# A four-layer graph kernel: later stages' constants are asked for later in the GpSimd queue

## The chip, the cores and the metric

The kernel runs on one core of one Trainium2 chip. A time is the device time of one execution in microseconds (us). Times of the kernel before are given as the median of three runs.

## The reference

There are 2708 tokens with 256 features and a dense 2708 x 2708 matrix `adj` with weights. Four layers follow one another, each of them a graph step and a feed-forward step, both added to `x`:

```
# layer 0
x = x + weights(adj) @ (layernorm(x) @ W + B)      # weight of an entry r: exp(-2 (1/r - 1)^2) where r < 1, else 0
x = x + top-2-of-8 experts(layernorm(x))           # gate: xf @ Wg + bg
# layer 1
x = x + relu(Dinv (adj + I) Dinv @ (layernorm(x) @ W) + b)
x = x + one-of-8 output experts(gelu(layernorm(x) @ W1 + b1))
# layer 2
x = x + elu(one-head attention over adj > 0: h = layernorm(x) @ W.T, scores from attn_src, attn_dst)
x = x + layernorm(two of 8 experts, the same for all tokens) with gamma, beta
# layer 3
x = x + elu(four-head attention over adj > 0, scores from a_l, a_r)
x = x + layernorm(x) @ weight.T + bias
```

All is float32.

## The kernel before

The tokens are 22 tiles of 128 rows (the last one has 20). `x` stays in on-chip memory throughout. A framework (Tile) takes the instructions in the order in which Python emits them, but it lays out the order of each engine's instructions itself, at compile time[...]. An instruction whose inputs are there may so be issued long before its neighbours in the source. `tc.add_manual_dep(... NoSync ...)` is a hint for this planner alone: "put this instruction behind that one on its engine's queue". [...]

**Queues.** Big loads (rows of `adj`, the weights of experts, `x`, `xT`) are asked for by SP (SyncE). Small constants, and all gathers and scatters of token rows (lines 505, 519 and 659), are asked for by GpSimd (POOL): `row_bc` (line 121) loads one vector of 256 numbers into all 128 partitions, 128 KB in all; `mat` (line 127) loads a small matrix. [...]

**The graph step of layer 0.** It begins the program. `centre(w_sb)` subtracts the column means from the layer's matrix (two products, four records on PE, lines 245 and 247). The output tokens are taken in three groups, `GROUPS`, of 9, 7 and 6 tiles. For each group and each of 21 row blocks j, SP loads a row block of `adjT` (`adrow`, line 903, five buffers), `weigh` turns it into weights `wt` with ScalarE and VectorE in turn (lines 141, 887 and 889; four buffers), and PE multiplies them with `msg` (line 931). In the first group, at each even j, `front(j)` also makes `msg` of two tiles: it loads their columns of `xT` (line 871, two buffers) and their rows of `x` (line 56), takes their mean and variance (lines 186 and 187), multiplies them by the layer's matrix (line 260) and writes `msg` (line 878). At j = 19 of the first group `last_rows` fills a buffer with ones on POOL (line 299) and loads the 20 last rows into it. `send` follows each group: it norms the tokens, takes the gate's product with `L0_ffn_Wg` (line 846) and `L0_ffn_bg` (line 848), and scatters the rows to their experts (line 505).

**The rest.** The experts of layer 0 run from about 270 us to 600 us. Layer 1 has the same shape (groups `GROUPS1`; `send1` writes each token's rank with a scatter, kept in `scattered["taken1"]`); its output experts are run by `work1` in blocks, each with a gather of names, a gather of rows, PE products (line 721), two VectorE instructions (lines 722 and 723) and a scatter into `given1`. `beside(b)` runs beside block b. At b = NA + 4 = 13 it asks for layer 2's constants `L2_gnn_attn_src`, `L2_gnn_attn_dst` and `w_l2`; at b = NA + 9 = 18 it notes the latest scatter as `work1.at_end`, and layer 2's other constants (`L2_ffn_Wr`, `br`, `b1`, `b2`, `gamma`, `beta`, and the matrix of layer 3) are put behind that scatter on POOL. Layer 2 then loads `given1` back (`mine`, line 56) once all scatters have landed. Layer 3's `a_r` and `a_l` are emitted in layer 2's first attention pass.

The constants of later stages that the source emits at the start, or that have no hint, are asked for by POOL as soon as their buffer is there.

Of the kernel before, what the change touches and what calls it, by code (L numbers as in the profile page):

```python
# [15 lines left out]
P = 128  # L16
N = 2708
D = 256
DC = D // P
E = 8  # L20
# [8 lines left out]
GROUPS = [range(0, 9), range(9, 16), range(16, NT)]  # L29
# [37 lines left out]
def adj_ffn4(ctx: ExitStack, tc: tile.TileContext, a: dict, out: bass.AP):  # L67
    nc = tc.nc
    v, s, g, te = nc.vector, nc.scalar, nc.gpsimd, nc.tensor
# [54 lines left out]
    def mat(pool, name, n):  # L124

        t = pool.tile([P, DC, n], F32, name=name, bufs=1)
        g.dma_start(t, a[name].rearrange("(c p) n -> p c n", p=P))
        return t
# [18 lines left out]
    def after(i, past):  # L147

        tc.add_manual_dep(i.ins, past, mybir.DependencyInfo(
            mybir.DependencyClass.NoSync, mybir.DependencyReason.DATA), reason="order")  # L150

    def in_order(first, engines):

        was = {}
        for i in nc.cur_bb.bb.instructions[first:]:
            if i.engine in engines:
                if i.engine in was:
                    tc.add_manual_dep(i, was[i.engine], mybir.DependencyInfo(
                        mybir.DependencyClass.NoSync, mybir.DependencyReason.DATA), reason="order")
                was[i.engine] = i.name  # L160
# [135 lines left out]

    def last_rows(dst, parts, filler):

        filler.memset(dst, 1.0)
        for q, k, c0, w in parts:  # L300
            nc.sync.dma_start(dst[q * Q : q * Q + LAST, k : k + w],
                              a["adjT"][FULL * P :, c0 : c0 + w])

    def last_product(p, q, weights, k, values, stop=True):
        te.matmul(p, lhsT=weights[q * Q : q * Q + LAST, k : k + P],
# [194 lines left out]
    scattered = {}  # L500
# [271 lines left out]
    ep = ctx.enter_context(tc.tile_pool(name="early", reuse_waits="tile", bufs=1))  # L772
# [14 lines left out]
    with ExitStack() as l0:  # L787
# [20 lines left out]
        w_sb = gp.tile([P, DC, D], F32, name="L0_gnn_W", bufs=1)  # L808
        first = nc.sync.dma_start(w_sb, a["L0_gnn_W"].rearrange("(c p) n -> p c n", p=P))
        b_bc = row_bc(gp, "L0_gnn_B", D)  # L810
        wg = mat(tp, "L0_ffn_Wg", E)
        bg = row_bc(tp, "L0_ffn_bg", E)
        w_l1 = mat(ep, "L1_gnn_W", D)
        b_l1 = row_bc(ep, "L1_gnn_b", D)
        choice = tp.tile([P, NT, 2], I32, name="choice", bufs=1)
        g.iota(choice, pattern=[[2 * P, NT], [1, 2]], base=0, channel_multiplier=2)
        msg = gp.tile([P, NT, D], F32, name="msg", bufs=1)
# [73 lines left out]
        for tiles in GROUPS:  # L891
            end = tiles is GROUPS[-1]
            own = [(t, (t - tiles[0]) * P, P) for t in tiles if t < FULL]
            c0, w = tiles[0] * P, own[-1][1] + P
            pairs = banks(tiles)
            acc = [gsum.tile([P, 2, D], F32, name="acc2", bufs=(GMAX + 1) // 2) for _ in pairs]

            places = {n: (n // 2 % 4, n // 8 * 2 + n % 2) for n in range(len(own))}
            begin = tiles is GROUPS[0]
            for j in range(FULL):  # L900
                r = rows(j)
                ad = gp.tile([P, GMAX * P], F32, name="adrow", bufs=5)[:r, :w]
                i = nc.sync.dma_start(ad, a["adjT"][j * P : j * P + r, c0 : c0 + w])
                after(i, reads[-1] if reads else first.ins.name)
                reads.append(i.ins.name)
                if begin and j % 2 == 0:
                    if j == 6:
                        centre(w_l1)
                    for t0 in (j,) if j < FULL - 3 else (j, j + 2) if j == FULL - 3 else ():
                        front(t0)  # L910
                if begin and j == FULL - 2:
                    spread_out(msg[:, FULL, :])
                if j == (FULL - 2 if begin else 12):
                    cols = [gp.tile([P, GMAX * P], F32, name=name, tag=name, bufs=bufs)[
                        :, : (1 + max(k for _, k in places.values())) * P]
                            for name, bufs in (("adrow", 5), ("y", 3), ("wt", 4))]
                    last_rows(cols[0], [(places[n][0], places[n][1] * P, c0 + n * P,
                                         min(2, len(own) - n) * P) for n in range(0, len(own), 2)], g)
                    weigh(*cols, P)
                    for n, t, _ in by_turns(own):  # L920
                        last_product(acc[n // 2][:, n % 2, :], places[n][0], cols[2],
                                     places[n][1] * P, msg[:, FULL, :], False)
                y = gp.tile([P, GMAX * P], F32, name="y", bufs=3)[:r, :w]
                wt = gp.tile([P, GMAX * P], F32, name="wt", bufs=4)[:r, :w]
                weigh(ad, y, wt, r)
                for p, pair in zip(acc, pairs):
                    for n in pair:
                        if n == len(own):
                            continue
                        _, k, q = own[n]  # L930
                        te.matmul(p[:q, n - pair[0], :], lhsT=wt[:, k : k + q],  # L931
                                  rhs=msg[:r, j, :], start=(j == 0 and n == pair[0]),
                                  stop=(j == FULL - 1 and n == pair[-1]))
                if end and j == 2:
                    cols = [gp.tile([P, GMAX * P], F32, name=name, tag=name, bufs=bufs)[
                        :, : NT * Q].rearrange("p (t c) -> p t c", c=Q)
                            for name, bufs in (("adrow", 5), ("y", 3), ("wt", 4))]
                    last_columns(cols[0])
                    weigh(*cols, P)
                    last = last_sums(acc[-1].rearrange("p k d -> p (k d)"), cols[2],  # L940
                                     lambda j, r: msg[:r, j, :], D)
                    v.tensor_tensor(x[:LAST, FULL, :], x[:LAST, FULL, :], last, ALU.add)
                if end and j == 0:
                    items = [(early, b, past0, taken[0][: 2 * held0], True) for b in range(N0)]
                    for item in items:
                        work0.fetch_rows(item)
                if end and j in (8, 14):
                    work0.fetch(items[j // 6 - 1])
                if end and j == NT - 5:
                    past = list(scattered["taken0"])  # L950
                    items += [(full, b, past, taken[0][: 2 * held], True) for b in range(NA - N0)]
            for p, pair in zip(acc, pairs):
                if pair[0] == len(own):
                    continue
                t, m, q = own[pair[0]][0], len(pair), own[pair[-1]][2]
                v.tensor_tensor(x[:q, t : t + m, :], x[:q, t : t + m, :], p[:q, :m, :], ALU.add)
            if end:
                sums.close()
                gnn.close()
                psum_pool(l0, 2, 3)  # L960
                hc = l0.enter_context(
                    tc.tile_pool(name="c0", side="right", reuse_waits="tile", bufs=1))
                hcs.append(hc)
                own_rows.append(behind_gate.enter_context(
                    tc.tile_pool(name="x0", reuse_waits="tile", bufs=1)))
                work0.late = hc
                work0.begun = work0.turn(hc, work0.rows[0])
                work0.made = work0.first_products(hc, work0.ahead[0], work0.begun, 2)
            send(tiles)
            if begin:  # L970
                early = blocks(hw, tp, known, N0, 2 * P, "E", full=True)
                past0 = list(scattered["taken0"])
            if tiles is GROUPS[-2]:
                full = blocks(hw, tp, known, NA - N0, 2 * P, "A", done=early[2], full=True)
# [10 lines left out]
        past = list(scattered["taken0"])  # L985
# [60 lines left out]
    with ExitStack() as l1:  # L1046
# [171 lines left out]
        def beside(b):  # L1218
            if b == NA + 9:
                work1.at_end = scattered["given1"][-1].name  # L1220
            if b == NA + 4:
# [5 lines left out]
                score_columns(w_l2, D, as_bc, 1, D)  # L1227
                score_columns(w_l2, D, ad_bc, 1, D + 1)
                centre(w_l2)
                for i in nc.cur_bb.bb.instructions[first:]:  # L1230
                    if i.engine in (mybir.EngineType.DVE, mybir.EngineType.PE):
                        tc.add_manual_dep(i, work1.last, mybir.DependencyInfo(
                            mybir.DependencyClass.NoSync, mybir.DependencyReason.DATA),
                            reason="order")

        work1 = Units(hw, given[1], weights1, hid)
        for tiles in GROUPS1:
# [138 lines left out]
    with tc.tile_pool(name="t3", reuse_waits="tile", bufs=1) as t3:  # L1376
# [34 lines left out]
        with tc.tile_pool(name="g2", reuse_waits="tile", bufs=1) as gp:  # L1411
# [110 lines left out]
            for n in (5, 5, 5, 4, 2):  # L1522
# [20 lines left out]
                if c0 == 0:  # L1543
# [1 line left out]
                    score_columns(wa, D, row_bc(work, "L3_gnn_a_r", D, "elu_e"), NH, D)  # L1545
                    score_columns(wa, D, row_bc(work, "L3_gnn_a_l", D, "elu_e"), NH, D + NH)
                    centre(wa)
                    for i in nc.cur_bb.bb.instructions[begin:]:
                        if i.engine == mybir.EngineType.DVE:
                            tc.add_manual_dep(i, spread, mybir.DependencyInfo(  # L1550
                                mybir.DependencyClass.NoSync, mybir.DependencyReason.DATA),
                                reason="order")

                    es = gp.tile([P, NT, Q], F32, name="es")
                    v.tensor_tensor(es[:, :FULL], Rb[:, None, N - Q : N].to_broadcast([P, FULL, Q]),
# [511 lines left out]
```

## Time and profile before

| | |
|---|---|
| median of 3 runs | 1903.86 us (1902.37 to 1904.59) |
| the profiled execution | 1902.01 us, its span 1900.2 us |
| PE (matmul) busy | 1821.4 us, 96% of the span |
| PE busy in 0 to 140 us, the first group | 128.36 us |
| PE busy in 1050 to 1080 us, the end of layer 1 | 19.62 us |
| POOL busy | 352.3 us, 19% |

Busy shares are averages over stages; the views of a stretch of time tell what a stage waits for. In a view by stretches each engine has its busy time and, in brackets, how many instructions began there; the last columns are the granted clock of TensorE, the busy share of the 16 DMA engines and the GB/s that they moved. Of the DMA queues, q1 holds what SP asks for and q0 what POOL asks for.

### The profile page before, as it was taken

How to read it: one execution, taken by the hardware profiler on the slowest of the kernel's cores; microseconds unless marked ns; L12 is line 12 of the kernel's file. 1: busy time of each engine (PE TensorE's matmuls, PEld its weight loads, DVE VectorE, ACT ScalarE, POOL GpSimd, SP SyncE). 2: the span in 40 equal slices, each digit the busy share in tenths (PEclk: the TensorE clock that was granted, in tenths of full speed). 3: DMA queues.
4: the chain of work that ended last, by engine and by line, in shares of the span. 5: the costliest groups of instructions: out<-in, count | busy, mean ns of one | idle time of the engine just before them, and what ended most of it. 6: DMA issues, size and time to landing. Idle time of an engine off the chain costs nothing.

```text
span 1900.2 us, 25781 instructions
## 1 busy us (share of the span) xinstructions
PE 1821.4 (96%) x9453; PEld 1325.5 (70%) x9453; DVE 1094.9 (58%) x2489; ACT 642.2 (34%) x1448; POOL 352.3 (19%) x415
## 2 busy tenths in 40 slices
PE   7999999999998999999989799998899999999998
PEld 6888788888887888887778688887566722232344
DVE  6777873443333524454532365555345499999897
ACT  7868752222223203022322232223233551131231
POOL 1004254333321002304356410000000000000000
PEclk9999999999998999999999899999899999999999
DMA  8435657877764453644777510000101000000000
GB/s 274 144 110 154 224 194 283 344 298 297 284 256 138 140 151 105 159 117 121 207 224 251 163 29 1 1 1 1 44 1 34 17 1 23 23 15 26 21 20 16
DMA packets 88846, 233.33 MB, mean 123 GB/s; under 512 B 18015, under 2 KB 44679, under 8 KB 80648
## 3 DMA queue, kind: packets, MB, share of 16 engines
q1 hardware_dynamic: 71752, 189.18, 30.4%
q0 software_dynamic: 16960, 42.42, 7.0%
q8 instruction: 78, 1.28, 0.3%
q14 instruction: 56, 0.46, 0.1%
HBM read 216.29 MB, written 28.71 MB: 129 GB/s over the span
## 4 chain that ended last, share of the span: by engine, by line
PE 39%; DVE 4%; DMA 4%; issue 1%; ACT 1%; POOL 1%; POOLq 0%; SPq 0%; DVEq 0%; ACTq 0%
PE num L1965 10%; PE ps_acc L1538 9%; PE den L1975 5%; PE ps_tmp L367 4%; PE ps_acc L1728 3%; PE yacc L721 2%; PE ps_tmp L260 2%; DVE e L1935 1%; DMA names<-taken,b_ix 1%; DMA L_ffn_beta<-in_L_ffn_beta 1%; PE ps_acc L260 1%; PE ps_acc L670 1%; DMA mine<-given 1%; PE ps_tmp L213 0%; DMA hs<-hid,names 0%
## 5 line engine op out<-in xcount | busy, mean ns | idle before, releaser
L1935 DVE SCALAR_TENSOR_TENSOR e<-arena,G,mask 128x1024 f32<-128x1024 f32 (+1 forms) x264 | 286.9, 1147 | 13.7 <-PE den L1975 13.6
L1965 PE MATMUL num<-e,wh 128*64 128x512 f32 (+4 forms) x1056 | 215.3, 551 | 0.3 <-ACT L_gnn_W L1358 0.3
L1538 PE MATMUL ps_acc<-hh,e 128*128 128x257 f32 x882 | 199.2, 382 | 1.7 <-ACT o L1481 1.7
L1302 PE MATMUL acc<-sup,adrow 128*128 128x256 f32 x882 | 199.6, 384 | 1.1 <-DVE adrow L1270 1.1
L931 PE MATMUL acc<-msg,wt 128*128 128x256 f32 x882 | 198.9, 382 | 1.3 <-DVE wt L889 1.2
L1302 PEld LDWEIGHTS acc<-sup,adrow 128*128 128x128 f32 x882 | 166.2, 191 | 29.0 <-issue 5.5
L931 PEld LDWEIGHTS acc<-msg,wt 128*128 128x128 f32 x882 | 165.8, 191 | 27.5 <-DVE wt L889 1.8
L1538 PEld LDWEIGHTS ps_acc<-hh,e 128*128 128x128 f32 x882 | 163.7, 190 | 29.2 <-ACT o L1481 4.3
L583 PE MATMUL ps_acc<-xTs,wa 128*128 128x256 f32 (+1 forms) x768 | 169.3, 373 | 2.1 <-DVE xTs L573 2.0
L617 PE MATMUL yacc<-wb,hTs 128*128 128x256 f32 x736 | 168.4, 380 | 0.0
L585 ACT ACTIVATE hTs<-ps_acc,wa 128x256 f32<-128x256 f32 (+1 forms) x192 | 88.9, 465 | 234.2 <-PE yacc L617 160.0
L583 PEld LDWEIGHTS ps_acc<-xTs,wa 128*128 128x128 f32 x768 | 136.4, 190 | 28.1 <-DVE xTs L573 4.5
L1965 PEld LDWEIGHTS num<-e,wh 128*64 128x64 f32 (+1 forms) x1056 | 66.6, 136 | 127.2 <-issue 105.0
L617 PEld LDWEIGHTS yacc<-wb,hTs 128*128 128x128 f32 x736 | 137.1, 190 | 17.9 <-DVE ys L619 0.5
L1530 DVE SCALAR_TENSOR_TENSOR e<-Rb,G,mask 128x640 f32<-128x640 f32 (+2 forms) x110 | 85.0, 775 | 91.0 <-PE ps_acc L1538 90.4
L1975 PE MATMUL den<-e,wh 128*32 128x512 f32 (+4 forms) x1056 | 118.0, 548 | 0.0
L1267 DVE TENSOR_SCALAR mask<-adrow 128x1024 uint8<-128x1024 f32 (+1 forms) x66 | 41.2, 625 | 122.6 <-DMA adrow<-in_adjT 122.2
L214 ACT COPY xT<-ps_tmp 128x256 f32<-128x256 f32 x76 | 26.8, 367 | 219.9 <-PE ps_tmp L213 219.7
L721 PE MATMUL yacc<-wb,hTs 128*128 128x256 f32 x384 | 87.8, 383 | 0.5 <-DMA wb<-in_L_ffn_Wdp 0.5
L889 DVE SCALAR_TENSOR_TENSOR wt<-adrow,wt 128x640 f32<-128x640 f32 (+3 forms) x67 | 71.0, 1063 | 26.8 <-ACT wt L141 26.4
L1975 PEld LDWEIGHTS den<-e,wh 128*32 128x32 f32 (+1 forms) x1056 | 30.2, 108 | 77.9 <-issue 73.8
L505 POOL DMA_INDIRECT given<-ys,xs x46 | 65.3, 1420 | 79.3 <-DVE ys L620 66.1
(464 smaller groups left out, 2581.8 us busy)
## 6 DMA issues: line engine op xcount, KB each, us to landing
adhalf<-in_adjT SPq DMA_DIRECT2D x42, 677.0 KB
wb<-in_L_ffn_W2p SPq DMA_DIRECT2D x24, 1152.0 KB
wb<-in_L_ffn_Wdp SPq DMA_DIRECT2D x24, 1152.0 KB
wa<-in_L_ffn_W1b SPq DMA_DIRECT2D x24, 1028.0 KB
adrow<-in_adjT SPq DMA_DIRECT2D x42, 512.0 KB
adrow<-in_adjT SPq DMA_DIRECT2D x42, 320.0 KB
adrow<-in_adjT SPq DMA_DIRECT2D x21, 576.0 KB
adrow<-in_adjT SPq DMA_DIRECT2D x21, 448.0 KB
```

Of the source, the lines that this page charges most:

```text
L367: te.matmul(p[:, :w], lhsT=w1[:, c, f * P : (f + 1) * P], rhs=xnT[:, c, c0 : c0 + w], start=(c == 0), stop=(c == DC - 1))
L583: i = te.matmul(p[:, f % 2, : m * P], lhsT=w1[:, c, f * P : (f + 1) * P], rhs=xT[:, c, : m * P], start=(c == 0), stop=(c == DC - 1))
L585: s.activation(hT[:, f, : m * P], p[:, f % 2, : m * P], AF.Gelu, bias=bias[:, f : f + 1])
L617: te.matmul(q[:, k, :], lhsT=hT[:, f, k * P : (k + 1) * P], rhs=w2[:, f, :], start=(f == 0), stop=(f == HC - 1))
L721: te.matmul(q, lhsT=hT[:, f, :], rhs=w2[:, f, :], start=(f == 0), stop=(f == HC - 1))
L931: te.matmul(p[:q, n - pair[0], :], lhsT=wt[:, k : k + q], rhs=msg[:r, j, :], start=(j == 0 and n == pair[0]), stop=(j == FULL - 1 and n == ...
L1302: te.matmul(p[:q, n - pair[0], :], lhsT=ad[:, k : k + q], rhs=sup[:, jj, :], start=(jj == 0 and n == pair[0]), stop=(jj == FULL - 1 and n ...
L1530: i = v.scalar_tensor_tensor(e[:r, :w], Rb[:r, c0 : c0 + w], G[:r, j, :], mask[:r, j, c0 : c0 + w], op0=ALU.max, op1=ALU.mult)
L1538: te.matmul(p[:, : D + 1], lhsT=e[:, k : k + q], rhs=hh[:, j, :], start=(j == 0), stop=False)
L1935: v.scalar_tensor_tensor(e[:, :w], slow[:, m % 2, k, :w], G[:, j, 2 * pair + k, :], mask[:, j, c0 : c0 + w], op0=ALU.max, op1=ALU.mult)
L1965: te.matmul(num[k * DK : (k + 1) * DK, hf, :q], lhsT=wh[some, j, 2 * pair + k, :DK], rhs=e[some, h0 - c0 : h0 - c0 + q], start=(j == 0), s ...
L1975: te.matmul(den[z : z + Q, :q], lhsT=wh[some, i, 2 * pair + k, DK : DK + 1] .to_broadcast([some.stop - some.start, Q]), rhs=e[some, h0 - c ...
```

## The change

A helper `engine_after(first, engine, past)` puts all instructions of one engine that were emitted since `first` behind the instruction `past`, with the same planner's hint. It is used to move nine loads of constants:

- `L0_ffn_Wg`, `L0_ffn_bg`, `L1_gnn_W` and `L1_gnn_b` are emitted at j = 19 of the first group and put behind the fill of `last_rows`, which now returns its name. `centre(w_l1)` moves from j = 6 of the first group to j = 6 of the second.
- `L2_gnn_attn_src`, `L2_gnn_attn_dst` and `w_l2` are put behind the first scatter of ranks of layer 1.
- `L3_gnn_a_r` and `L3_gnn_a_l` are put behind `work1.at_end`.

```
+    def engine_after(first, engine, past):
+
+        for i in nc.cur_bb.bb.instructions[first:]:
+            if i.engine == engine:
+                tc.add_manual_dep(i, past, mybir.DependencyInfo(
+                    mybir.DependencyClass.NoSync, mybir.DependencyReason.DATA), reason="order")
...
     def last_rows(dst, parts, filler):
 
-        filler.memset(dst, 1.0)
+        i = filler.memset(dst, 1.0)
...
+        return i.ins.name
...
         b_bc = row_bc(gp, "L0_gnn_B", D)
-        wg = mat(tp, "L0_ffn_Wg", E)
-        bg = row_bc(tp, "L0_ffn_bg", E)
-        w_l1 = mat(ep, "L1_gnn_W", D)
-        b_l1 = row_bc(ep, "L1_gnn_b", D)
...
+                if tiles is GROUPS[1] and j == 6:
+                    centre(w_l1)
                 if begin and j % 2 == 0:
-                    if j == 6:
-                        centre(w_l1)
...
-                    last_rows(cols[0], ...)
+                    filled = last_rows(cols[0], ...)
+                    if begin:
+                        later = len(nc.cur_bb.bb.instructions)
+                        wg = mat(tp, "L0_ffn_Wg", E)
+                        bg = row_bc(tp, "L0_ffn_bg", E)
+                        w_l1 = mat(ep, "L1_gnn_W", D)
+                        b_l1 = row_bc(ep, "L1_gnn_b", D)
+                        engine_after(later, mybir.EngineType.Pool, filled)
...
-                for i in nc.cur_bb.bb.instructions[first:]:
-                    if i.engine in (mybir.EngineType.DVE, mybir.EngineType.PE):
...
+                for e in (mybir.EngineType.DVE, mybir.EngineType.PE):
+                    engine_after(first, e, work1.last)
+                engine_after(first, mybir.EngineType.Pool, scattered["taken1"][0].name)
...
-                    for i in nc.cur_bb.bb.instructions[begin:]:
-                        if i.engine == mybir.EngineType.DVE:
...
+                    engine_after(begin, mybir.EngineType.DVE, spread)
+                    engine_after(begin, mybir.EngineType.Pool, work1.at_end)
```

More of the change, by code (lines that the diff above doesn't have):

```diff
@@ L916, in adj_ffn4 @@
                             for name, bufs in (("adrow", 5), ("y", 3), ("wt", 4))]
-                    last_rows(cols[0], [(places[n][0], places[n][1] * P, c0 + n * P,
-                                         min(2, len(own) - n) * P) for n in range(0, len(own), 2)], g)
+                    filled = last_rows(cols[0], [(places[n][0], places[n][1] * P, c0 + n * P,
+                                                  min(2, len(own) - n) * P)
+                                                 for n in range(0, len(own), 2)], g)
+                    if begin:
[5 more added lines that the diff above has]
+                        engine_after(later, mybir.EngineType.Pool, filled)
                     weigh(*cols, P)
@@ L1229, in beside @@
                 centre(w_l2)
-                for i in nc.cur_bb.bb.instructions[first:]:
-                    if i.engine in (mybir.EngineType.DVE, mybir.EngineType.PE):
-                        tc.add_manual_dep(i, work1.last, mybir.DependencyInfo(
-                            mybir.DependencyClass.NoSync, mybir.DependencyReason.DATA),
-                            reason="order")
+                for e in (mybir.EngineType.DVE, mybir.EngineType.PE):
+                    engine_after(first, e, work1.last)
+                engine_after(first, mybir.EngineType.Pool, scattered["taken1"][0].name)
         work1 = Units(hw, given[1], weights1, hid)
@@ L1547, in adj_ffn4 @@
                     centre(wa)
-                    for i in nc.cur_bb.bb.instructions[begin:]:
-                        if i.engine == mybir.EngineType.DVE:
-                            tc.add_manual_dep(i, spread, mybir.DependencyInfo(
-                                mybir.DependencyClass.NoSync, mybir.DependencyReason.DATA),
-                                reason="order")
+                    engine_after(begin, mybir.EngineType.DVE, spread)
+                    engine_after(begin, mybir.EngineType.Pool, work1.at_end)
                     es = gp.tile([P, NT, Q], F32, name="es")
```

## The prediction

> **What bounds the kernel now.** I read the page first, then PE's waits, then the stretches of time around the places that the nine moved loads leave and go to. The page says that PE is the engine to watch:
>
> ```profile
> PE 1821.4 (96%) x9453; PEld 1325.5 (70%) x9453; DVE 1094.9 (58%) x2489; ACT 642.2 (34%) x1448; POOL 352.3 (19%) x415
> ```
>
> Only PE's idle time can be won, 79 us of the span. The loads leave the first ten microseconds, so I asked for PE's waits in 0 to 140 us (line, releaser, us in total, times, longest):
>
> ```profile
> PE ps_tmp L260 <- DMA xT<-in_xT: 6.9, 1, 6.9
> PE ps_tmp L245 <- DMA L_gnn_W<-in_L_gnn_W: 3.8, 1, 3.8
> ```
>
> One wait of 6.9 us stands out: the first products of tiles 2 and 3 wait for their columns of `xT`. Next the stretches of 5 us (PE, PEld, DVE, ACT, POOL busy, clock, DMA share, GB/s):
>
> ```profile
> 0.00:5.00 5.00, 1.25 (x3) 1.10 (x4) 0.82 (x28) 1.28 (x1) 4.34 (x15) 1.00 0.55 194
> 5.00:10.00 5.00, 4.48 (x10) 2.60 (x9) 1.56 (x6) 2.42 (x2) 2.91 (x7) 1.00 0.98 282
> 10.00:15.00 5.00, 0.10 (x1) 0.00 (x0) 4.42 (x14) 4.48 (x6) 0.00 (x0) 1.00 0.99 328
> 15.00:20.00 5.00, 3.05 (x7) 2.51 (x8) 3.24 (x6) 2.85 (x3) 0.00 (x0) 1.00 1.02 392
> 20.00:25.00 5.00, 5.00 (x18) 4.11 (x18) 3.64 (x5) 5.00 (x8) 0.00 (x0) 1.00 0.89 274
> ```
>
> From 5 to 20 us the DMA engines are full, and PE does 7.6 us of work in 15. From 20 us on PE is full; from 20 to 200 us it is idle for 0.6 us. So the program's head is bound by DMA, and what follows by PE. Who uses the full DMA engines? The queue rows (packets, MB, share), of 5 to 10 us and then of 10 to 15 us:
>
> ```profile
> q1 hardware_dynamic: 595, 1.10, 59.8%
> q0 software_dynamic: 153, 0.31, 38.5%
> ```
>
> ```profile
> q0 software_dynamic: 294, 0.85, 54.6%
> q1 hardware_dynamic: 408, 0.79, 44.9%
> ```
>
> POOL's constants (q0) take over two fifths of the engines just when SP's loads (q1) are late.
>
> [...]the two shares above add up to 98% and 99.5%. [...]q0 has 38% to 55% while q1 has a backlog. [...]The trace has records of line 931 of 634 ns at first and 379 ns later; I use it only as an upside.
>
> **Part 1: the start.** Eight of POOL's early loads go: `Wg` 8 KB, `bg` 4, `L1_gnn_W` 256, `L1_gnn_b` 128, `attn_src` 128, `attn_dst` 128, `w_l2` 256, `a_r` 128: 1036 of 1164 KB. `L_gnn_B` (128 KB) stays. q0's engine time: 5 us x 0.385 + 5 x 0.546 + 5 x 0.034 (its share in 15 to 20 us) = 4.83 us. Taken by bytes, 1036/1164 of it are **4.3 us** of full DMA service, all before the `xT` transfer lands at 16.95. So it lands near 12.6.
>
> Check from SP's side. By 16.95 us q1 had moved 0.97 + 1.10 + 0.79 + some 0.75 (1.95 us at 15 to 20's rate) = 3.6 MB; what was asked for up to this transfer is 2.75 MB (matrix 256, three `adrow` of 576, two `xT` and one `x` of 256 KB). At 380 KB/us behind the 0.97 MB of the first 5 us, and with `L_gnn_B` beside, it lands between 5 + (1.78 + 0.13)/0.38 = 10.0 and 5 + (2.63 + 0.13)/0.38 = 12.3. So this wait of 6.9 us, which began at 10.1, shrinks to between 0 and 2.5 us: 4.4 to 6.9 us won there.
>
> What is late next: the first weights `wt`, for the sum of j = 0, which PE began at 20.52 after the products of tiles 2 and 3. `wt` was ready at 14.8, through rows that wait for loads: stats on `x` at 9.19, the second `adrow` at 11.01, then ScalarE 12.18 to 13.4 and VectorE 13.45 to 14.8. With these loads 1.5 to 2 us earlier, it is ready near 13. The products of tiles 2 and 3 last 3.78 us from 11 to 12.6, to 14.8 to 16.4: they remain last, so the sum begins 4.1 to 5.7 us earlier. The next weights were ready at 22.7 and needed at 26.13, and come 3 to 3.5 us earlier, needed 5 earlier: still ahead. After that VectorE waits for PE to free `wt` buffers (7 times, 8.7 us in 0 to 140), so PE sets the pace and the shift stays. Upside: [...](up to 1.4 us: the first 18 records of line 931 took 5.12 us, later ones 3.75). I take **4.7 us** won, bounds 3 and 7.
>
> **Part 2: the four loads behind the fill.** POOL's rows there:
>
> ```profile
> 81.26 0.41 POOL L299 MEMSET adrow<- 128x384 f32 x1 [71.81 <-DMA xT<-in_xT]
> 138.88 4.54 POOL L835 COPY xr<-xr 128x256 f32<-128x256 f32 x9 [57.20 <-DVE xr L197]
> ```
>
> Four issues at 0.58 to 0.74 us are 2.6 us of POOL in a pause of 57 us; nothing is queued behind them there. At the 8.6 us that `L_gnn_b` took from issue to landing at the full start, they land by 93 us; `Wg` is read at 140.5. The DMA share in 80 to 90 us is 0.33, so 396 KB (1 us) cost nothing; cover: SP's row blocks are prefetched five deep. `centre(w_l1)` costs PE four records, 1.03 us, and VectorE 0.76 us, in the first group or in the second: PE is full in both, so 0, bounds -0.5 and +1.
>
> **Part 3: three loads behind layer 1's first rank scatter.** That scatter is at 780.02; the eight end at 790.6, one small copy follows at 798.82, and the next POOL work is at 846.76. Three issues, 1.9 us, lie in this pause, or between scatters whose rows are first gathered at 911.95. 512 KB cost 1.3 us of DMA where its share is about 0.5. PE is idle for only 1.2 us in 700 to 900, so row blocks come early enough. So 0. The data are read at 1021. SP's requests are untouched.
>
> **Part 4: `a_r` and `a_l` behind `work1.at_end`.** This is the tightest place:
>
> ```profile
> 1051.86 0.79 POOL L127 DMA_DIRECT2D L_ffn_Wr<-in_L_ffn_Wr  x1
> ...
> 1062.76 0.99 POOL L505 DMA_INDIRECT given<-xn,names  x1 [2.06 <-DVE xn L723]
> 1067.09 0.98 POOL L505 DMA_INDIRECT given<-xn,names  x1 [3.34 <-DVE xn L723]
> 1070.55 0.98 POOL L505 DMA_INDIRECT given<-xn,names  x1 [2.47 <-DVE xn L723]
> ```
>
> The last scatter ends the path: all of layer 2 waits for it. Seven constants are issued in 1051.86 to 1058. Two more at 0.6 us, 1.2 us (one is new here, `a_l` moves from 1033), delay the scatters queued behind them (1058.35, 1059.69), but the last three waited 2.06, 3.34 and 2.47 us for VectorE: hidden. If the planner puts both right ahead of the last scatter, up to 1.2 us. Expected 0.2, bounds 0 and 1.2. They are read at 1133.
>
> **Sum.** -4.7 + 0 + 0 + 0.2 = -4.5 us. Against the profiled execution's 1902.01: 1897.5. The median of the runs stands 1.85 us above that execution, so 1903.86 - 4.5 = **1899.4 us**, 0.24% less. A measurement of this kernel can tell about 0.2%, 3.8 us, from no change.
>
> **Rivals.** *The gain is there but small* (0.27): `xT` lands earlier by q0's time, yet the transfers are bound by request order or the weights become last, and the later issues take something back: 3 - 1 = 2 us, 1901.9. [...]Against: engine shares near 1 at the start.
>
> *The planner's new order costs more* (0.12): [...]The third pair's `xT` waits for a buffer until the first pair's products end (SP's request is at 10.13), which costs little: about 16 + 3.8 = 19.8, a gain of 0.7. The fourth pair's can be asked for only when the second pair's end, near 15, and takes some 8 us (13.1 before, less 5): sums from 23 + 2 to 23 + 3.8, 4.5 to 6.3 us later than 20.5. That point, the fourth pair ahead of the first sum, decides: 1909. For it: this order is fixed at compile time and has no hint. Against: the order before had one pair ahead only.
>
> *The loads don't move as said* (0.03): the fill is planned near the start, and the four behind it stay early: 640 of 1036 KB go, 2.9 us, 1901.
>
> **The numbers.** The likeliest case has 0.58, at 1899.4, nearly all of it below the 0.2% line with its upside. The others give mostly no difference and the third case slower: faster 0.57, same 0.30, slower 0.13. The range reaches from 1895.8 [...]to 1905, which leaves out most of the slower case.
>
> **What would show it.** Right: in the profile after, q0 is nearly empty in 5 to 15 us, PE's wait for `xT` falls below 3 us, the first record of line 931 begins at 14.5 to 16.5, group ends move by the same, and the last scatter still waits for VectorE. Wrong: this record at 19 or later, PE idle in 20 to 140 us above 2 us, or POOL late at the end of layer 1.

## The result and the profile after

The changed kernel takes **1898.21 us** (median of 11 runs, 1895.86 to 1902.76) where the kernel before took 1903.96 in the same comparison (11 runs). The ratio is 0.9971, 95% interval 0.9961 to 0.9982: 3.4 to 7.4 us less. The profiled execution of it took 1896.49 us, its span is 1894.8.

The page's engine line, the one that was shown of before, has the same instruction counts; PE is busy 2.4 us less in a span that is 5.4 us shorter, so more than half of the gain is idle time of PE:

```profile
PE 1819.0 (96%) x9453; PEld 1325.1 (70%) x9453; DVE 1094.6 (58%) x2489; ACT 640.6 (34%) x1448; POOL 353.5 (19%) x415
```

PE's waits in 0 to 140 us of the changed kernel (line, releaser, us in total, times, longest):

```profile
PE ps_tmp L267 <- DMA xT<-in_xT: 3.9, 2, 2.9
PE ps_tmp L252 <- DMA L_gnn_W<-in_L_gnn_W: 3.8, 1, 3.8
```

The wait for `xT` is 3.9 us where it was 6.9, now in two pieces. PE's own rows at the start of the changed kernel (start, us, instruction, idle before it):

```profile
8.75 3.75 PE L267 MATMUL ps_tmp<-L_gnn_W,xT 128*128 128x256 f32 x8 [2.86 <-DMA xT<-in_xT]
13.53 3.78 PE L267 MATMUL ps_tmp<-L_gnn_W,xT 128*128 128x256 f32 x8 [1.04 <-DMA xT<-in_xT]
17.11 4.21 PE L943 MATMUL acc<-msg,wt 128*128 128x256 f32 x18
```

The products of tiles 2 and 3 start at 13.53 (16.95 before), the first weighted sum (line 943, which was 931) at 17.11 (20.52 before). That is 3.4 us earlier. The stretches of 5 us (PE, PEld, DVE, ACT, POOL busy, clock, DMA share, GB/s; an instruction that crosses a bound is counted in both stretches):

```profile
5.00:10.00 5.00, 2.14 (x6) 1.27 (x5) 0.75 (x2) 2.42 (x2) 0.00 (x0) 1.00 0.87 236
10.00:15.00 5.00, 3.96 (x10) 2.59 (x10) 4.79 (x15) 3.93 (x6) 0.00 (x0) 1.00 1.04 411
15.00:20.00 5.00, 5.00 (x19) 4.23 (x18) 4.14 (x8) 4.97 (x6) 0.00 (x0) 1.00 0.97 335
```

The DMA engines move 411 GB/s in 10 to 15 us (328 before), and PE is full from 15 us, not from 20. But in 5 to 10 us they moved only 236 GB/s. The queue rows for 5 to 10 us (packets, MB, share) say what was in the way:

```profile
q1 hardware_dynamic: 588, 1.05, 56.9%
q0 software_dynamic: 48, 0.13, 29.7%
```

All of q0 here is `L_gnn_B`, the one constant that stayed. It takes 29.7% of 5 us, 1.5 us of all engines, for 0.13 MB. From 10 to 15 us q0 has no row.

The four loads behind the fill stand where they were meant to, and POOL has nothing else until 133 us (two of the four are shown):

```profile
75.61 0.42 POOL L306 MEMSET adrow<- 128x384 f32 x1 [72.43 <-DMA xT<-in_xT]
75.97 0.77 POOL L127 DMA_DIRECT2D L_ffn_Wg<-in_L_ffn_Wg  x1
...
77.99 0.55 POOL L121 DMA_DIRECT2D L_gnn_b<-in_L_gnn_b  x1
133.23 4.53 POOL L839 COPY xr<-xr 128x256 f32<-128x256 f32 x9 [54.68 <-DVE xr L204]
```

At the end of layer 1 POOL's rows are (with the two moved loads, and the last three scatters):

```profile
1049.77 0.55 POOL L121 DMA_DIRECT2D L_gnn_a_r<-in_L_gnn_a_r  x1 [0.24 <-DMA L_ffn_Wr<-in_L_ffn_Wr]
1050.39 0.54 POOL L121 DMA_DIRECT2D L_gnn_a_l<-in_L_gnn_a_l  x1
...
1057.47 0.98 POOL L513 DMA_INDIRECT given<-xn,names  x1 [3.31 <-DVE xn L731]
1061.80 0.98 POOL L513 DMA_INDIRECT given<-xn,names  x1 [3.34 <-DVE xn L731]
1065.25 0.98 POOL L513 DMA_INDIRECT given<-xn,names  x1 [2.47 <-DVE xn L731]
```

The last scatter comes 5.3 us earlier than before (1070.55) and waits for VectorE the same 2.47 us. Between these two places one thing is new, a wait of PE near 800 us (PE's rows, then the stretches of 4 us around it):

```profile
790.72 7.17 PE L1312 MATMUL acc<-sup,adrow 128*128 128x256 f32 x32
800.05 6.31 PE L1312 MATMUL acc<-sup,adrow 128*128 128x256 f32 x28 [2.16 <-DMA adrow<-in_adjT]
```

```profile
790.00:794.00 4.00, 4.00 (x28) 3.27 (x21) 2.58 (x6) 0.00 (x0) 0.54 (x1) 1.00 0.99 122
794.00:798.00 4.00, 3.90 (x19) 3.08 (x17) 0.35 (x2) 0.00 (x0) 0.00 (x0) 1.00 1.00 263
798.00:802.00 4.00, 1.95 (x9) 1.74 (x10) 1.83 (x4) 0.00 (x0) 0.00 (x0) 1.00 0.88 348
```

The three loads are issued at 787.21, 787.79 and 788.35. In 790 to 794 the DMA engines are full (0.99) and move 122 GB/s, where before they moved 183 at 0.81; `adrow` then comes late and PE is idle for half of 798 to 802.

**The lead by places.** PE's order is nearly the same in both kernels, so the same matmul can be looked up in both. The table gives how much earlier it starts than in the profile of the kernel before. Columns are times of that profile in us; in the first column it is the first weighted sum, at 20.52. The rows of the experiments are read below.

| profile | 20 | 150 | 190 | 240 | 590 | 640 | 790 | 810 | 1030 | 1890 |
|---|---|---|---|---|---|---|---|---|---|---|
| changed | 3.4 | 5.6 | 4.8 | 3.7 | 2.7 | 3.3 | 3.4 | 2.1 | 5.3 | 5.4 |
| before, again (`b0_before`) | -0.7 | -0.5 | -0.5 | -1.7 | -4.2 | -4.7 | -4.5 | -4.9 | -0.7 | -2.6 |
| changed, again (`e0_again`) | 4.0 | 6.4 | 5.6 | 5.4 | 4.7 | 4.9 | 5.0 | 4.6 | 8.6 | 7.4 |
| `e2_again` | 5.4 | 6.3 | 5.5 | 4.8 | 3.8 | 3.6 | 3.7 | 3.5 | 4.4 | 4.0 |
| `e5_vectors_early` | 3.5 | 5.9 | 5.1 | 4.1 | 2.2 | 3.1 | 3.3 | 3.4 | 5.0 | 3.2 |
| `e6_matrix_early` | 4.8 | 5.7 | 4.9 | 3.6 | 1.7 | 1.6 | 1.7 | 1.8 | 2.0 | 0.1 |
| `e7_centre_late` | 6.0 | 6.9 | 6.9 | 5.7 | 4.1 | 3.0 | 3.1 | 2.3 | 4.7 | 4.4 |
| `e8_fill_and_centre` | 5.9 | 6.9 | 6.9 | 5.8 | 4.7 | 1.9 | 2.3 | 2.9 | 5.7 | 4.3 |
| `e4_b_by_row` | 6.3 | 1.8 | 0.9 | 0.3 | -1.2 | -1.1 | -0.9 | -1.9 | 0.1 | -1.3 |
| changed, other chip (`e0_after`) | 5.2 | 4.9 | 4.0 | 3.8 | -8.9 | -8.2 | -8.1 | -8.2 | -7.1 | -8.8 |

Of the change itself: **+4.8 us** at 190 us (5.3 against the second profile of before), all from the head, and **-1.3** between 790 and 810. Just behind 190 us the first profile after loses 1.1 us in a wait for VectorE at the end of the second group (1.2 us); `b0_before` has this wait too (1.3), so it isn't put down to the change. The +3.2 between 810 and 1030 isn't the change's: before, again, gains 4.2 there against its own other profile. Single profiles of one kernel differ by some 4 us behind 240 us, so the table is read only at steps that several rows share.

### The profile page after: what moved, and what is told of

It reads as the page before. It is cut to its first block, busy times and chain, and to the rows that moved or that the text cites. A ratio compares the mean times of both kernels' runs of the same rounds, so it can differ in the third digit from the quotient of the medians.

```text
span 1894.8 us, 25782 instructions
## 1 busy us (share of the span) xinstructions
PE 1819.0 (96%) x9453; PEld 1325.1 (70%) x9453; DVE 1094.6 (58%) x2489; ACT 640.6 (34%) x1448; POOL 353.5 (19%) x415
## 4 chain that ended last, share of the span: by engine, by line
PE 40%; DVE 4%; DMA 3%; ACT 1%; issue 1%; POOL 1%; SPq 0%; POOLq 0%; DVEq 0%; ACTq 0%
PE num L1972 10%; PE ps_acc L1548 9%; PE den L1982 5%; PE ps_tmp L375 4%; PE ps_acc L1735 3%; PE yacc L729 3%; PE ps_tmp L267 2%; DVE e L1942 1%; DMA L_gnn_a_r<-in_L_gnn_a_r 1%; PE ps_acc L678 1%; PE ps_acc L267 1%; DMA mine<-given 1%; PE ps_tmp L220 0%; DMA hs<-hid,names 0%; DMA taken<-names,r_ix 0%
```

## The experiments

Theory (mine): the lead comes from the DMA engines at the head, and the rank stage at 790 us gives some back. Rivals: the gain belongs to single runs; the planner's order, not the DMA, decides; or the place of single loads matters little. There were three comparisons, each on one chip. The first was on another chip than the two others; its kernel before took 1917.12 us, against 1902.61 and 1901.17. The figures of single places are each from one profile.

### The changed kernel again, and its parts (first comparison)

`e0_after` is the changed kernel, unedited.

> The changed kernel once more, to see which of its places repeat. Mine: the head (first record of the weighted sums at 17.1 us, where it was 20.5 before) and PE's wait of about 2.2 us for adrow near 797 us, behind the three loads at layer 1's ranks, repeat within 0.3 us; the 2 to 3 us that the changed kernel won in 1010 to 1025 us, at the gathers of layer 1's end, do not repeat as such, being chance of when gathers land. Total about 0.3% below before. Rival: the end's gain belongs to the change (a_l has left the run of gathers) and repeats within 0.5 us.

Measured 1916.16 us, ratio 0.9995 (0.9984 to 1.0005): no difference that can be told. The forecasts missed: the first sum came at 15.34 instead of 17.1, the wait near 800 us was 0.9 us instead of 2.2, and no gain of 0.3% was seen. Only the end's gain shrank as expected, from 3.2 to 1.1 us. The head's lead was there, but in this profile 2.0 us of it go between 240 and 288 us and 9.7 us more by 300, in layer 0's experts. One wait of PE in 210 to 300 us belongs to it (line, releaser, us in total, times, longest):

```profile
PE yacc L625 <- DVE ys L627: 6.9, 1, 6.9
```

All four profiles of this comparison have this wait, of 4.4 to 7.0 us; the first two profiles, of before and after, `e0_again` and `e7_centre_late` don't have it. Between 240 and 590 us this profile loses 12.6 us of its lead, and those of the three other kernels of this comparison lose 12.6 to 15.1; no profile of the two other comparisons loses more than 2.5 there, and that of the same changed kernel, `e0_again`, loses 0.7. So the loss was seen on this chip alone. The kernel before is itself 14 us slower here, which would fit the same loss. But it wasn't profiled on this chip, so how much of it it pays, and why the gain isn't seen here, stays open.

`e1_first_only` keeps only the four loads behind the fill:

```
-                engine_after(first, mybir.EngineType.Pool, scattered["taken1"][0].name)
...
-                    engine_after(begin, mybir.EngineType.Pool, work1.at_end)
```

> Only the four loads of layer 0 and 1 are behind the fill; the two attn vectors, w_l2 and a_r are asked for at the start again (640 of 1036 KB), a_l near 1030 us. Mine: the first weighted sum begins late again, at 18.5 to 20 us (17.1 with the whole change, 20.5 before); no wait for adrow near 797 us, 2.2 us won back there; so the total is within 1.5 us of the changed kernel. Rival (bytes alone decide, broadcast or not): 396/1036 of the 3.4 us, first sum at 19.2. Rival (a_l's move pays at the end of layer 1): 2 us more are lost at 1010 to 1050, the total is 2 to 3 us above the changed kernel.

Measured 1917.28 us, ratio 0.9999 (0.9989 to 1.0009). The planner puts `attn_src`, `attn_dst`, `w_l2` and `a_r` back at the start, and q0 has 44.4% of 5 to 10 us and 29.8% of 10 to 15. PE's row for tiles 2 and 3 and the first sum behind it:

```profile
14.95 3.78 PE L267 MATMUL ps_tmp<-L_gnn_W,xT 128*128 128x256 f32 x8 [4.95 <-DMA xT<-in_xT]
18.52 4.73 PE L943 MATMUL acc<-msg,wt 128*128 128x256 f32 x18
```

The wait goes down to 4.95 us and the first sum comes 2.0 us earlier than before: a part of the loads brings a part of the lead, as expected. The rival that counts bytes alone (19.2) is only 0.7 us away, less than three profiles of the changed kernel differ by (1.8), so this doesn't separate them. PE does not wait for `adrow` near 800 us, as these three loads aren't there.

`e2_behind_fill` asks for these three behind the fill too (`early_fill` holds the fill's name):

```
-                engine_after(first, mybir.EngineType.Pool, scattered["taken1"][0].name)
+                engine_after(first, mybir.EngineType.Pool, early_fill[0])
```

> The two attn vectors and w_l2 also go behind the fill at 75 us instead of behind layer 1's first rank scatter; all else as changed. Mine: the head stays (first sum at 17.1), PE's wait of 2.2 us for adrow near 797 us goes, and 900 KB at 76 to 82 us cost PE nothing or up to 1 us, since row blocks are prefetched: 1 to 2 us faster than the changed kernel, 1896 to 1897. Rival (that wait has another cause, the row block would be late anyway): the wait stays, total as the changed kernel. Rival (the same loads hurt wherever they go): a wait of about 2 us for adrow near 85 us instead.

Measured 1911.84 us, ratio 0.9975 (0.9965 to 0.9984), 4.3 us below the changed kernel beside it; first sum at 14.75, no wait for a transfer behind the fill, and a wait of 0.5 us for `adrow` near 804 (0.9 beside it, in `e0_after`): it shrank and didn't go. The gain is more than the wait taken away, so it was run again below.

`e3_no_end_hint` leaves the planner free with `a_r` and `a_l`:

```
-                    engine_after(begin, mybir.EngineType.Pool, work1.at_end)
```

> a_r and a_l have no hint: a_r is asked for behind the rank scatters near 789 us with the three others, a_l in the run of gathers near 1030 us. Mine: the wait for adrow near 797 us grows from 2.2 to about 3 us (a third broadcast vector), nothing changes at the last scatter, which waits for VectorE for 2 to 3 us either way: total 0 to 1 us above the changed kernel. Rival (a_l in the run of gathers is what cost the kernel before 2 to 3 us): PE waits for hs again in 1010 to 1050 us, total 2 to 4 us above.

Measured 1915.66 us, ratio 0.9997 (0.9985 to 1.0009), 0.5 us from the changed kernel. `a_r` becomes a fourth load behind the rank scatters, and the wait for `adrow` there grows to 2.9 us (0.9 beside it). The tail is as before: the last scatter still waited 2.47 us. No gain from the place of `a_l` can be told.

### Which load costs (second comparison)

`b0_before` is the kernel before, unedited, for a second profile.

> The kernel before itself, for a profile on the same chip as the three others of this call. All theories: ratio 1.000; the first weighted sum begins near 20.5 us (within 1.5), POOL's queue has 35 to 55% of the DMA engines in 5 to 15 us, and no wait for adrow over 1 us in 780 to 830 us. It shows whether what follows the first 260 us differs between kernels or between chips.

Measured 1903.29 us, ratio 0.9995 (0.9983 to 1.0007). Its first sum starts at 21.22, 0.7 us from the first profile; PE waits 8.1 us for `xT`, in two pieces. So the start of the first pair's products (6.3 us or 9.1 us) varies in the kernel before as it does after, and the first piece, of 2.86 us, in the changed kernel's profile is no cost of the change.

`e5_vectors_early` takes the hint from the two attention vectors, `e6_matrix_early` from `w_l2` (each is 256 KB in all):

```
# e5: only what follows the vectors is hinted
+                matrix = len(nc.cur_bb.bb.instructions)
...
-                engine_after(first, mybir.EngineType.Pool, scattered["taken1"][0].name)
+                engine_after(matrix, mybir.EngineType.Pool, scattered["taken1"][0].name)
# e6: the hint stands ahead of the matrix
+                engine_after(first, mybir.EngineType.Pool, scattered["taken1"][0].name)
...
-                engine_after(first, mybir.EngineType.Pool, scattered["taken1"][0].name)
```

> The changed kernel with L2_gnn_attn_src and attn_dst (two vectors, each loaded into all 128 partitions: 256 KB) asked for at the start again. Mine (a vector that is spread to 128 partitions holds the DMA engines several times longer than its bytes say: L_gnn_B took 1.2 to 1.5 us of all engines for 0.13 MB): 2.5 to 3 us of engine time more, the first weighted sum begins 1.5 to 3 us later than in the changed kernel. Rival (bytes alone count): 256 KB are 0.7 us, the sum begins 0.3 to 0.7 us later, as with the matrix. Both: less wait for adrow near 797 us, as only w_l2 is asked for there; mine says none, the rival half.

> The changed kernel with the matrix w_l2 (256 KB as well, every partition its own rows) asked for at the start again. Mine: 0.7 us of engine time, the first weighted sum begins at most 0.8 us later than in the changed kernel; the wait for adrow near 797 us stays at 1 to 2 us, since the two vectors are asked for there. Rival (bytes alone): the same 0.3 to 0.7 us as with the two vectors, and the wait near 797 us is halved.

Measured 1898.44 us (ratio 0.9973, 0.9963 to 0.9983) and 1899.38 us (0.9982, 0.9971 to 0.9994). First sums at 16.98 and 15.77, both inside the 15.3 to 17.1 of the changed kernel's three profiles: at the head 256 KB more can't be told apart. My 1.5 to 3 us for the vectors were wrong, and the rival that counts bytes is nearer: q0 takes 2.07 us of all engines in 5 to 15 us with the vectors (5 x 0.382 + 5 x 0.031) and 2.06 with the matrix, where the changed kernel has 1.49. Either 256 KB cost 0.6 us there. So that a row is spread to 128 partitions doesn't by itself explain the 1.5 us of `L_gnn_B`; what makes this one dear was not separated. Near 792 us both show a wait of 0.2 us; that a wait would be left with the vectors alone was wrong too.

What differs more is q0's price at the ranks, in 787 to 799 us, in which the loads land whole (packets, MB, share of 12 us), here of the changed kernel, then of the one with the matrix alone (`e5_vectors_early`), then of the one with the vectors alone (`e6_matrix_early`):

```profile
q0 software_dynamic: 282, 0.53, 43.7%
```

```profile
q0 software_dynamic: 164, 0.27, 6.7%
```

```profile
q0 software_dynamic: 192, 0.27, 12.3%
```

The matrix takes 0.8 us of all engines (12 x 0.067) for 0.27 MB, the vectors 1.5 us for 0.27 MB, and the three together 5.2 us for 0.53 MB. That is 3.0, 5.5 and 9.9 us for a MB: here the three together cost more than twice the sum of the two parts. Being together isn't the whole cause, though. Behind the fill the same three loads stand together as well, and there q0 has these rows in 74 to 86 us, of `e2_again` and of the changed kernel, which has only the other four loads there:

```profile
q0 software_dynamic: 368, 0.93, 29.2%
```

```profile
q0 software_dynamic: 192, 0.41, 14.9%
```

The difference is 1.7 us (12 x 0.143) for 0.52 MB: the same loads cost a third of what they cost at the ranks. Why is open.

`e4_b_by_row` loads `L_gnn_B` as one row of 1 KB and spreads it by a product with ones:

```
-        b_bc = row_bc(gp, "L0_gnn_B", D)
+        b_row = gp.tile([1, D], F32, name="b_row", bufs=1)
+        g.dma_start(b_row, ...)
+        b_bc = gp.tile([P, D], F32, name="L0_gnn_B", bufs=1)
...
+        p = ps_tmp()
+        te.matmul(p[:, :D], lhsT=all_ones[:1, :], rhs=b_row, start=True, stop=True)
+        s.copy(b_bc, p[:, :D])
```

> The changed kernel with L_gnn_B loaded as one row of 1 KB and spread by a product with ones on PE (a copy on ScalarE after it). Mine: the gap in 5.5 to 8 us, where the engines are busy and move under 100 GB/s, goes; xT of the first pair lands 1 to 2 us earlier, and so does the first weighted sum or more; total 1 to 3 us below the changed kernel. Rival (the gap is HBM or the start of SP's queue, not the vector): the gap stays, nothing is won, the added product and copy cost 0.3 us.

Measured 1906.89 us, ratio 1.0016 (1.0006 to 1.0026): 4.3 us slower than the kernel before, where a time below the changed kernel was expected. The transfers did what was wanted. Queue rows of 5 to 10 us:

```profile
q1 hardware_dynamic: 1038, 1.90, 103.7%
q0 software_dynamic: 32, 0.00, 0.4%
```

q1 moves 1.90 MB instead of 1.05. But the planner's order changes with the edit, and PE's rows show the rest:

```profile
14.27 11.05 PE L949 MATMUL acc<-msg,wt 128*128 128x256 f32 x36 [3.59 <-DVE msg L888]
25.16 1.89 PE L267 MATMUL ps_tmp<-L_gnn_W,xT 128*128 128x256 f32 x8
```

```profile
10.00:15.00 5.00, 1.41 (x5) 0.92 (x4) 4.13 (x7) 5.00 (x6) 0.00 (x0) 0.86 1.06 411
15.00:20.00 5.00, 5.00 (x14) 3.92 (x13) 5.00 (x7) 5.00 (x7) 0.00 (x0) 0.50 0.68 217
```

The sums start at 14.27, 2.8 us ahead of the changed kernel, but behind a pause of 3.6 us in which PE waited for `msg`. The clock is then 0.50 in 15 to 20 us, and 36 records take 11.05 us; at the changed kernel's 4.21 us for 18 they would take 8.4. The clock is back at 0.96 in 20 to 25 us. Behind the 4.86 us for which PE waited in `b0_before` it is 0.50 too (17.5 to 22.5 us), but behind the 6.85 us in the first profile of before it is 1.00. At 150 us the lead is 1.8 us, 3.8 less than the changed kernel's. The slow records are 2.6 us, the larger part of what is lost, and another 1.7 us goes between 70 and 130 us, where the clock of 110 to 120 us is 0.83. `e0_after`, `e1_first_only` and `e3_no_end_hint` show such a dip too (0.83 to 0.87), so it isn't this edit alone.

### Is there a better version (third comparison)

The changed kernel and `e2_behind_fill` once more, unedited:

> The changed kernel once more, for the others of this comparison to stand against. Mine: ratio to the kernel before between 0.9965 and 1.0000 (0 to 6.6 us less), first record of the first group's sums at 14.7 to 17.2 us, and again a wait of PE for adrow of 0.9 to 2.5 us just behind 797 us. Rival (the gain belongs to single runs, not to the change): ratio 0.9990 to 1.0010.

> The three loads of layer 1's first rank scatter stand behind the fill instead, once more, to see whether the 4.3 us below the changed kernel of the first comparison come back. Mine: no wait for adrow behind 797 us, so 0.9 to 2.2 us less than the changed kernel; the rest of the 4.3 us was spread of the gathers. Rival A (the place of these loads is worth more than the wait that the trace shows): again 3.5 us or more below the changed kernel. Rival B (the stall is made up for later): within 0.6 us of the changed kernel.

Measured 1896.04 us (ratio 0.9973, 0.9962 to 0.9984) and 1896.93 us (0.9976, 0.9966 to 0.9986). The gain of the change repeats on this chip. The 4.3 us of `e2_behind_fill` don't: it is now 0.9 us above the changed kernel, which can't be told from none. Rival B is nearest. The wait for `adrow` is there in the first (1.3 us) and nearly gone in the second (0.3), and their ends don't show it: 1.3 us is less than what a comparison tells.

`e7_centre_late` moves the centring; `e8_fill_and_centre` has both edits:

```
-                if tiles is GROUPS[1] and j == 6:
-                    centre(w_l1)
...
+        centre(w_l1)
         project(gp, w_l1, deg, both,
```

> The changed kernel with the centring of layer 1's matrix moved from the second token group to just ahead of layer 1's products. Mine (the step costs PE 1.0 us of records wherever it stands, and in the second group another 1.1 us at the group's end, where PE waits for VectorE): the matmuls of groups 2 to 4 start 2.0 us earlier than in the changed kernel, layer 1's products give 1.0 us back and perhaps 0.5 more, since PE then waits for the centred matrix: 0.5 to 1.0 us less in all. Rival (PE waits in front of layer 1's products for the centred matrix, which goes through PE, VectorE and ScalarE): 1 us more than the changed kernel.

> Both: the three loads behind the fill, and the centring just ahead of layer 1's products. Mine: the sum of the two before, 1.4 to 3.2 us less than the changed kernel and so below both kernels (ratio to the kernel before 0.9955 to 0.9985). Rival (what is won ahead of layer 1 is taken back by waits for gathers of layer 1): within 0.6 us of the changed kernel.

Measured 1897.63 us (ratio 0.9982, 0.9969 to 0.9994) and 1896.64 us (0.9975, 0.9964 to 0.9985). In the table the lead doesn't drop by 0.8 to 0.9 us between 150 and 190 us, as it does wherever the centring stands in the second group. But between 590 and 640 us 1.1 and 2.8 us are lost, where the changed kernel's two profiles gain 0.6 and 0.2: four records of 2.07 us in all stand on PE's path there. So all of it is given back, or more. My 2.0 us was wrong in its second half: PE's wait for VectorE at the second group's end (1.4 us here) stays without the centring, and `b0_before` has it too, at 1.3 us. Of `e8_fill_and_centre` 1.4 to 3.2 us less were expected; it is 0.6 us above the changed kernel, so the rival holds. No version can be told to beat the changed kernel.

## Why the prediction was right

The forecast was 1899.4 us and faster; measured was 1898.21, and 0.9971. Point by point:

- **What bounds the head**: right. The wait of tiles 2 and 3 for `xT` (6.9, 5.0 and 1.0 us) and q0's share of 10 to 15 us (54.6%, 29.8% and none) go down together from the kernel before by way of `e1_first_only` to the changed kernel, in which PE is full from 15 us on.
- **q0's 4.83 us, "taken by bytes", 4.3 freed**: too large. `L_gnn_B`, which stays, takes 1.5 us and not the 0.5 that its bytes give, so 4.83 - 1.5 = 3.3 us came free. The products of tiles 2 and 3 start 3.4 us earlier, at 13.53; the text had `xT` landing between 10.0 and 12.6.
- **First sum at 14.5 to 16.5, 4.1 to 5.7 us earlier**: it was 17.11 in the profile after, and 16.48 and 15.34 in the two others. The order of what is late next was right: the products stayed last. Of the other signs of being right, the wait for `xT` is 3.9 us and not below 3, and q0 is empty from 10 us on but not before. No sign of being wrong came: PE is idle for 0.5 us in 20 to 140 us.
- **4.7 us won at the head**: 4.8 at 190 us, but by other terms: 3.4 from the transfers, 0.9 from the first sums (18 records in 4.21 us, 5.12 before, at a granted clock of 1.00 in both; why was not shown), which the text had only as an upside, and 0.5 more by 70 us.
- **Centring moved, 0**: right. It is some 0.9 us of lead, won in the first group and given back in the second.
- **Four loads behind the fill, 0**: right; no wait of PE appears behind them.
- **Three loads behind the rank scatter, 0**: wrong. The step that failed is "512 KB cost 1.3 us of DMA where its share is about 0.5", an estimate (the 392 GB/s of 15 to 20 us before give it). They took 4.6 to 5.2 us of all engines in three profiles of the changed kernel, and the share was an average: in the kernel before it is already 0.81 in 790 to 794 us and 1.20 in 794 to 798. That PE was idle for little in 700 to 900 us said nothing of the slack in the row blocks. Measured: a wait of 0.9 to 2.2 us, and a lead lower by 0.4 and 1.3 us at 810 than at 790 in `e0_again` and in the first profile after.
- **`a_r` and `a_l`, 0.2**: right in kind; the last scatter waits for VectorE by the same 2.47 us, and `e3_no_end_hint` ends alike.
- **The sum**: +4.8 - 1.3 = 3.5 us by the trace, where the two profiled executions differ by 5.5 (1902.01 to 1896.49) and the medians by 5.75. The difference lies in stages whose spread without any change is as large. So the mechanism was right, but that the sum came within 1.2 us of the forecast is in part luck: the freed DMA time was put too high, the faster first sums were not counted, and the loss at the ranks was put at nothing.
- **The rivals**: the planner's order is out for this change, since PE's order differs in eight of 9453 records (the four of the centring and four products beside them), that of SP's loads in none. In `e4_b_by_row` the order did change with the edit, and the time was 4.3 us above that of the kernel before, though q1 moved 1.90 MB in 5 to 10 us (1.05 in the changed kernel). "The gain is small" would fit the first comparison alone.

## What to carry to other kernels

Take loads that aren't needed early out of the first microseconds where PE waits for a transfer, and price them by the engine time that their queue takes in that stretch, not by bytes: one vector of 128 KB took 1.5 us here, two more beside it 0.6, and the same three loads 5.2 us in one place and 1.7 in another. Where they go, look at the DMA share of those few microseconds, not at the stage's mean. When PE must pause, look at the granted clock behind the pause as well: it was 0.50 for 5 us behind a pause of 3.6 us in `e4_b_by_row`, and 1.00 behind 6.85 us in the first profile of before. And measure a gain on a second chip: in the third comparison the change won 5.1 us, in the first none could be told.

## What was not expected of the hardware

- Full engines moved little at one place: 122 GB/s at a share of 0.99 (790 to 794 us, changed kernel), against 411 GB/s at 1.04 in 10 to 15 us. The slow stretch has two 128 KB vectors in it, the same row for each of 128 partitions, beside a matrix and `adrow`. The three loads took 5.2 us there; the two parts alone took 0.8 and 1.5, and all three behind the fill 1.7. Neither the spread rows nor standing together explains this by itself, and the cause was not separated.
- The same eight products took 3.78 us behind a pause of 1.04 us (changed kernel) and 1.99 us behind one of 1.60 us (`e6_matrix_early`), both at a granted clock of 1.00 in the trace. So the clock in the trace doesn't tell the two apart, and the cause was not shown.
- A granted clock of 0.83 to 0.87 in 110 to 120 us appears in `e0_after`, `e1_first_only`, `e3_no_end_hint` and `e4_b_by_row`; it is 1.00 there in the first two profiles, of before and after, in `e0_again` and in `e2_behind_fill`. In `e4_b_by_row` 1.7 us of lead go between 70 and 130 us.
- A wait of PE of 4.4 to 7.0 us in layer 0's experts is in all four profiles of the first comparison, with four different kernels. The changed kernel met it on that chip (6.9 us, `e0_after`) and not on the other one (`e0_again`).
